# A 64-wide inversion level in three batches instead of four, and a normalisation taken off GpSimd

## The chip, the cores and the metric

The kernel runs on one core of a Trainium2 chip. The metric is device time in microseconds, the median of the runs shown. One further execution was profiled; its trace is what the prediction reads. In the profile, PE is TensorE's matmuls and PEld its weight loads, DVE is VectorE, ACT is ScalarE, POOL is GpSimd.

## The reference

Two transformer layers with a layer norm after each of their four parts. The first layer is grouped-query attention with rotary positions and a gated feed-forward block, over 2 sequences of 1024 tokens of width 256. The second layer is a gated delta rule with 16 heads of width 128, and a feed-forward block with sign weights. The change touches the delta rule alone:

```python
def step(S, inp):
    qt, kt, vt, at, bt = inp
    err = jnp.einsum('bhvk,bhk->bhv', S, kt) - vt
    S = at[..., None, None] * S - bt[..., None, None] * err[..., None] * kt[:, :, None, :]
    o = jnp.einsum('bhvk,bhk->bhv', S, qt)
    return (S, o)
...
mu = o.mean(-1, keepdims=True)
var = ((o - mu) ** 2).mean(-1, keepdims=True)
o = (o - mu) * jax.lax.rsqrt(var + 1e-05) * ln_w + ln_b
g = jax.nn.sigmoid(x @ Wg).reshape(B, T, H, DV)
o = (o * g).reshape(B, T, H * DV)
return o @ Wo
```

## The kernel before

The delta rule is computed in chunks of 128 tokens. Inside a chunk, the recurrence becomes the inverse of a unit triangular 128x128 matrix (`lt` in the code), and between chunks a 128x128 state `M` is carried. The tokens are cut into four stretches of 512 (`HT`), which the code calls halves because two of them make a sequence; the heads are taken in pairs. One **step** `i` of the main loop is one stretch and one pair of heads: 4 chunks x 2 heads, so `U` = 8 triangular matrices. There are 4 x 8 = 32 steps, i = 0 to 31. The attention layer and the first feed-forward block come before them, the last feed-forward block is mixed into the last two steps.

**Order of the work.** A step is 120 units long (`UNIT`). Each part of the work is a generator that yields the unit at which its next piece is due, and `Places.run` always continues the piece that is due first. From step 0 on (`te.strict`), every matmul is tied to the one before it by `te.link`, so TensorE's order is exactly this order. On the other engines a list scheduler at build time picks among the instructions that its own timeline believes ready, by priority: the order of emission, with what stands under `tc.high_priority()` first. What comes out is a fixed queue for each engine. On the chip each engine runs its queue in order.

**The chain, `recur(i)`.** For each of the 4 chunks: at unit 0 of 30 the product `pr` (lines 657 and 661; 661 needs `M`), a copy `prs` on ACT (line 664); at unit 10 the product `pw` with the inverse `lt` (line 672) and the copy `wc` on ACT (line 675); at unit 20 `pm` (line 684), from which DVE makes the new `M` (lines 689 and 691), and `po` (lines 699 and 700), which ACT copies to `o` (line 703). The PSUM pool of the chain has two banks, so the next `pr` also needs DVE to have read `pm`.

**The fill.** Between these pieces TensorE runs the projections of the next steps (`pp`, lines 932 to 934), the transposes and score products, and the inversion: `keys` builds `lt` (product `pkk`, line 338, at units 131 and 141, that is units 11 and 21 of the following step), `blocks` solves the 16x16 blocks, and `levels(i)` puts them together, for two steps (16 matrices) at a time. It runs once every two steps, from step 1 on for i = 2, 4, ... 30: 15 times. One more, `levels(0)`, is emitted ahead of step 0, where the order of matmuls isn't tied yet.

**The last level** joins two 64x64 inverses into one of 128x128. With `A` the first 64 partitions and `Z` the last 64, it is a first product `p3` (rows `A` of the array, columns `Z`; line 469), its negated copy `n3` on ACT (line 471), a second product `p4` (rows `Z`, columns `A`; line 476), and a copy of `p4` into `lt` on ACT (line 477). It is done for one step's 8 matrices after the other's, at units 103, 113, 132 and 142 of the step in which `levels` runs; 132 and 142 lie in the next step. The last four `AT_LEVELS` are these units. `levels` has a PSUM pool of one bank from step 0 on (`"l"`, 1 buffer); `levels(0)` has one with two.

**The normalisation, `finish(i)`.** It runs in the step after. At unit 3 comes the reciprocal root: a few operations on DVE, then 12 small ones on POOL (lines 905 to 908), then `nb` on DVE (line 587). Each of 8 tiles `o` of 128x128 is normalised by one instruction; the string `NORM` says where: `P` POOL, `D` DVE (both line 597), `A` ACT (line 594). At units 41 and 51 TensorE transposes the normalised tiles (`pt`, line 603), first those of head 0 (tiles 0, 2, 4, 6). The last step has a string of its own, `NORM_LAST`.

Of the kernel before, what the change touches and what calls it, by code (L numbers as in the profile page):

```python
# [11 lines left out]
F32 = mybir.dt.float32  # L12
# [3 lines left out]
AF = mybir.ActivationFunctionType  # L16
ALU = mybir.AluOpType
# [3 lines left out]
P = 128  # L21
# [17 lines left out]
U = HP * HC  # L39
# [39 lines left out]
START = 29  # L79
RAW = 4  # L80

NORM, NORM_LAST = 'PDAPDAPD', 'DDADADAA'

UNIT, GAP = 120, 10
AT_ROWS, AT_QUERIES, AT_KC, AT_GATE, AT_GATE_ROWS, AT_SCORES = 1, 31, (42, 52), 61, 70.5, (71, 81)
AT_OUT = 9.5
AT_KEYS, AT_DECAY, AT_TRIANGLE = 91, 113, (131, 141, 146)
AT_BLOCKS, BLOCK_STEP = (44, 52, 145), 2.2
AT_LEVELS = 43, 53, 73, 83, 103, 113, 132, 142
AT_FFN = 24  # L90
AT_FINISH, AT_FINISH_LAST, AT_HALF = (41, 51, 101, 111), (31, 41, 71, 76), ((22, 30, 46), (12, 18, 36))

# [52 lines left out]
def delta_rule(  # L145
# [13 lines left out]
    nc = tc.nc  # L159
# [3 lines left out]
    early = open_pool(left, "dearly", "left", 2)  # L163
# [21 lines left out]
    def bank(pool, tag, name):  # L185
        return pool.tile([P, HT], F32, name=name, tag=tag)
# [43 lines left out]
    st = [dict() for _ in range(B * 2 * NS)]  # L230
# [4 lines left out]
    def place(i):  # L235

        return divmod(i, NS)
# [172 lines left out]
    def levels(i, psum):  # L410

        dd = st[i]["dd"]
        quarter = [slice(q * BL, (q + 1) * BL) for q in range(Q)]
        p0 = bank(*psum, "p0").rearrange("p (u t) -> p u t", t=BL)
        with tc.high_priority():
            for v in range(2 * U):
                for r in quarter:
                    te.link(nc.tensor.matmul(p0[r, v, :], lhsT=lo[r, v, :], rhs=dd[r, v, :], start=True, stop=True))
        n0 = early.tile([P, 2 * U, BL], F32, name="n0", tag="tt", bufs=1)
        with tc.high_priority():  # L420
            nc.vector.scalar_tensor_tensor(
                n0, p0, -1.0, ib.unsqueeze(1).to_broadcast([P, 2 * U, BL]), ALU.mult, ALU.add
            )
        yield AT_LEVELS[1]
        px = bank(*psum, "px").rearrange("p (u t) -> p u t", t=BL)
        with tc.high_priority():
            for v in range(2 * U):
                for r in quarter:
                    te.link(nc.tensor.matmul(px[r, v, :], lhsT=dt[r, v, :], rhs=n0[r, v, :], start=True, stop=True))
        nc.scalar.copy(X[0 : 3 * BL, :, 0:BL], px[0 : 3 * BL])  # L430
        nc.scalar.copy(X[quarter[1], :, BL : 2 * BL], px[quarter[1]])

        with tc.high_priority():
            nc.vector.transpose(dd.rearrange("p u t -> p (u t)"), px.rearrange("p u t -> p (u t)"))
        for n in range(2):
            for r in quarter:
                (nc.gpsimd.tensor_copy if n else nc.scalar.copy)(
                    st[i + n]["lt"][r, :, r], dd[r, n * U : (n + 1) * U]
                )
        yield AT_LEVELS[2]  # L440
        b0, b1, b2, b3 = [slice(q * BL, (q + 1) * BL) for q in range(Q)]
        A, Z = slice(0, 64), slice(64, 128)
        us = [(n * U + u, st[i + n]["lt"], u) for n in range(2) for u in range(U)]
        p1 = bank(*psum, "p1").rearrange("p (u t) -> p u t", t=BL)
        with tc.high_priority():
            for v, lt, u in us:
                te.link(nc.tensor.matmul(p1[b1, v, :], lhsT=lt[b0, u, b1], rhs=X[b0, v, 0:BL], start=True, stop=True))
                te.link(nc.tensor.matmul(p1[b3, v, :], lhsT=lt[b2, u, b3], rhs=X[b2, v, 0:BL], start=True, stop=True))
        n1 = early.tile([P, 2 * U, BL], F32, name="n1", tag="tt", bufs=1)
        for r in (b1, b3):  # L450
            nc.scalar.activation(n1[r], p1[r], AF.Copy, scale=-1.0)
        yield AT_LEVELS[3]
        p2 = bank(*psum, "p2").rearrange("p (u t) -> p u t", t=BL)
        with tc.high_priority():
            for v, lt, u in us:
                te.link(nc.tensor.matmul(p2[b0, v, :], lhsT=n1[b1, v, :], rhs=lt[b1, u, b1], start=True, stop=True))
                te.link(nc.tensor.matmul(p2[b1, v, :], lhsT=lt[b1, u, b1], rhs=n1[b1, v, :], start=True, stop=True))
                te.link(nc.tensor.matmul(p2[b2, v, :], lhsT=n1[b3, v, :], rhs=lt[b3, u, b3], start=True, stop=True))
        nc.vector.tensor_copy(X[b1, :, 0:BL], p2[b1])
        for n in range(2):  # L460
            lt = st[i + n]["lt"]
            nc.scalar.copy(lt[b0, :, b1], p2[b0, n * U : (n + 1) * U])
            nc.scalar.copy(lt[b2, :, b3], p2[b2, n * U : (n + 1) * U])
        for n in range(2):
            yield AT_LEVELS[4 + 2 * n]
            p3 = bank(*psum, "p3").rearrange("p (u t) -> p u t", t=64)
            with tc.high_priority():
                for v, lt, u in us[n * U : (n + 1) * U]:
                    te.link(nc.tensor.matmul(p3[Z, u, :], lhsT=lt[A, u, Z], rhs=X[A, v, :], start=True, stop=True))  # L469
            n3 = early.tile([P, U, 64], F32, name="n3", tag="n3", bufs=1)  # L470
            nc.scalar.activation(n3[Z], p3[Z], AF.Copy, scale=-1.0)
            yield AT_LEVELS[5 + 2 * n]
            p4 = bank(*psum, "p4").rearrange("p (u t) -> p u t", t=64)
            with tc.high_priority():
                for v, lt, u in us[n * U : (n + 1) * U]:
                    te.link(nc.tensor.matmul(p4[A, u, :], lhsT=n3[Z, u, :], rhs=lt[Z, u, Z], start=True, stop=True))  # L476
            nc.scalar.copy(st[i + n]["lt"][A, :, Z], p4[A])

    def pair(m, i):

# [86 lines left out]
    def finish(i, o, m, chunks, places):  # L567
# [5 lines left out]
        if chunks[0] == 0:  # L573
            st[i]["wo"] = []
            for part in range(2):
                t = pools["late"].tile([P, HP, E], F32R, name=f"wo{part}", tag=f"wo{part}", bufs=1)
# [11 lines left out]
        for c in chunks:  # L588
            for h in range(HP):
                n = (c - c1) * HP + h  # L590
                oc, r1 = o[:, c, h, :], rs[:, n : n + 1]
                how = (NORM if i < last else NORM_LAST)[n]
                if how == "A":
                    nc.scalar.activation(oc, oc, AF.Identity, bias=nb[:, n : n + 1], scale=r1)
                else:
                    eng = nc.gpsimd if how == "P" else nc.vector
                    eng.tensor_scalar(oc, oc, m[:, n, 0:1], r1, ALU.subtract, ALU.mult)
        ys = []
        for h in range(HP):
            yield places[h]  # L600
# [12 lines left out]
        for c0 in range(0, nc_, 2):  # L613
            yield places[2 + c0 // 2]
            pf = bank(pools["t"], "t", "pf").rearrange("p (c e) -> p c e", e=E)
            for c in range(2):
                for h in range(HP):
                    t = slice((c0 + c) * P, (c0 + c + 1) * P)
# [10 lines left out]
    def recur(i):  # L629
# [8 lines left out]
        def moments(c):  # L638
            for h in range(HP):
                st6 = pools["late"].tile([P, 6], F32, name="ost", tag="ost")  # L640
                nc.vector.bn_stats(st6, o[:, c, h, :])
                nc.vector.bn_aggr(m[:, c * HP + h, 0:2], st6)
            part = HC // 2 if i == last else HC
            if c % part == part - 1:
                chunks = range(c + 1 - part, c + 1)
                at = i * UNIT + 3 * GAP * (c + 1) + 3
                lines.add(finish(
                    i, o, m[:, chunks[0] * HP : (c + 1) * HP, :], chunks,
                    AT_HALF[c // part] if i == last else AT_FINISH_LAST if i == last - 1 else AT_FINISH,
                ), at, at if i == last else (i + 1) * UNIT)  # L650
# [160 lines left out]
    for i in range(-AHEAD, last + 1):  # L811
        te.strict = i >= 0
        t = i * UNIT
# [4 lines left out]
        if i == -1:  # L818
            drain(keys(3, 0))
            drain(levels(0, (ps_m, "m")))  # L820
            open_late()
# [12 lines left out]
        if i >= 0:  # L834
            lines.add(recur(i), t, chain=True)
            if i % 2 == 0 and i + 2 <= last:
                lines.add(blocks(i + 2, (pools["l"], "l")), t + AT_BLOCKS[0], t)
            if i % 2 == 1 and i + 1 <= last:
                lines.add(levels(i + 1, (pools["l"], "l")), t + AT_LEVELS[0], t)
        hi, s = place(i + AHEAD + 1)  # L840
# [809 lines left out]
```

## Time and profile before

| | |
|---|---|
| runs | median 2069.81 us of 3 (2068.07 to 2072.84) |
| profiled execution | 2075.78 us, of which the span from first to last instruction is 2074.1 us |
| granted TensorE clock, mean over the span | 0.975 |
| PE / PEld busy | 1897.8 us (92%) / 1496.0 us (72%) |
| DVE / ACT / POOL busy | 1493.4 us (72%) / 1269.6 us (61%) / 1035.4 us (50%) |
| step 0 begins / last matmul of the last `levels` starts | 822.7 us / 1920.8 us |

Rows of the timeline are: start, duration (both in us), engine, line, operation, output tile <- input tiles, shape, count, and in brackets the idle time of the engine just before, with what ended it. Buffer numbers are left out of names, so `p3` and `p4` are both `p`, `n3` is `n`, and the blocks of the inverse are `ll`. A float32 matmul shows as two instructions: 8 products are 16 rows.

### The profile page before, as it was taken

What the parts mean: (1) busy time and instruction counts of PE and PEld (TensorE: products, weight loads), DVE (VectorE), ACT (ScalarE), POOL (GpSimd) and SP (SyncE); (2) the same over time, 40 slices, a digit from 0 to 9 for tenths busy, and PEclk for the clock granted to TensorE, in tenths of its full rate; (3) what the DMA queues carried; (4) which work ended last, traced back from release to release, by engine and by line L of the source; (5) the groups of instructions that cost most, each with busy time, mean ns of one, the idle gap of its engine ahead of it and who ended that gap; (6) DMA issues with size and microseconds to landing.
All of it is one profiled execution on the core that took longest, in us unless ns stands there. A gap on an engine that the chain in (4) does not pass through costs nothing.

```text
span 2074.1 us, 49172 instructions
## 1 busy us (share of the span) xinstructions
PE 1897.8 (92%) x18657; PEld 1496.0 (72%) x18657; DVE 1493.4 (72%) x3629; ACT 1269.6 (61%) x2731; POOL 1035.4 (50%) x1539
## 2 busy tenths in 40 slices
PE   5898889999998888899999999998999999999896
PEld 3454455555555777788889888887888888888775
DVE  6755666877757896477786887778678678775576
ACT  1365556576755355567667676766677666676532
POOL 4353333331123453566776656666567676565430
PEclk9999999999999998999999999999999999999997
DMA  5563444442132422443443534444434444443010
GB/s 173 173 185 119 148 127 127 144 135 69 52 76 62 120 74 53 126 129 107 120 132 99 157 99 116 116 122 127 112 114 128 122 115 128 108 132 89 21 41 21
DMA packets 312997, 229.16 MB, mean 110 GB/s; under 512 B 139640, under 2 KB 278904, under 8 KB 312760
## 3 DMA queue, kind: packets, MB, share of 16 engines
q1 hardware_dynamic: 299640, 210.73, 35.0%
q10 hardware_dynamic: 9760, 10.83, 1.6%
q0 software_dynamic: 3360, 4.46, 0.9%
q8 instruction: 147, 2.41, 0.5%
q14 instruction: 90, 0.74, 0.1%
HBM read 171.18 MB, written 51.87 MB: 108 GB/s over the span
## 4 chain that ended last, share of the span: by engine, by line
PE 58%; DVE 13%; ACT 6%; DMA 5%; issue 3%; POOL 2%; SPq 1%; ACTq 0%; POOLq 0%; DVEq 0%
PE pp L932 5%; PE pp L934 4%; PE pp L933 4%; PE ps L1306 4%; PE av L1327 4%; PE ps L1237 3%; PE pkq L506 3%; PE pm L684 2%; DVE at L325 2%; PE pw L672 2%; PE pr L661 2%; PE po L700 2%; PE po L699 2%; PE p L476 2%; PE p L469 2%
## 5 line engine op out<-in xcount | busy, mean ns | idle before, releaser
L1246 DVE TENSOR_REDUCE mx<-ps 128x4 f32<-128x1024 f32 (+1 forms) x320 | 344.3, 1111 | 135.2 <-PE ps L1237 91.2
L1310 ACT ACTIVATE es<-ps 128x512 f32<-128x512 f32 (+1 forms) x608 | 314.0, 577 | 130.2 <-PE ps L1306 119.5
L1306 PE MATMUL ps<-qT,kT 128*128 128x512 f32 (+3 forms) x768 | 221.5, 372 | 21.9 <-ACT es L1310 20.6
L1237 PE MATMUL ps<-kT,qT 128*128 128x512 f32 x576 | 198.8, 419 | 27.8 <-DVE mx L1246 18.7
L1306 PEld LDWEIGHTS ps<-qT,kT 128*128 128x128 f32 x768 | 131.4, 191 | 107.9 <-ACT es L1310 61.5
L1237 PEld LDWEIGHTS ps<-kT,qT 128*128 128x128 f32 x576 | 101.0, 189 | 87.8 <-DVE mx L1246 48.1
L289 ACT ACTIVATE far<-pp,cw 128x509 f32<-128x509 f32 x192 | 133.2, 699 | 47.1 <-DVE v L275 20.8
L1327 PE MATMUL av<-es,vaug 128*32 128x512 f32 (+3 forms) x1536 | 159.4, 503 | 0.2 <-POOL es L1313 0.2
L882 POOL TENSOR_TENSOR wfl<-wf,wfh 128x256 fp32r<-128x256 f32 x80 | 58.6, 734 | 191.0 <-ACT wfh L970 163.0
L1313 POOL TENSOR_SCALAR_AFFINE_SELECT es<-es 128x512 f32<-128x512 f32 x128 | 80.4, 638 | 146.3 <-ACT es L1310 146.1
L275 DVE SCALAR_TENSOR_TENSOR k<-pp,cw,k 128x511 f32<-128x511 f32 (+1 forms) x128 | 92.0, 743 | 46.7 <-ACT k L268 25.0
L275 DVE SCALAR_TENSOR_TENSOR q<-pp,cw,q 128x511 f32<-128x511 f32 (+1 forms) x128 | 93.0, 742 | 45.1 <-ACT q L268 22.2
L292 POOL TENSOR_TENSOR q<-q,far 128x509 f32<-128x509 f32 x64 | 69.4, 1087 | 97.4 <-ACT far L289 97.2
L275 DVE SCALAR_TENSOR_TENSOR v<-pp,cw,v 128x511 f32<-128x511 f32 (+1 forms) x128 | 92.3, 739 | 30.7 <-ACT v L268 18.3
L292 POOL TENSOR_TENSOR k<-k,far 128x509 f32<-128x509 f32 x64 | 78.4, 1227 | 56.8 <-ACT far L289 56.4
L516 POOL TENSOR_TENSOR k<-k,dg 128x508 f32<-128x508 f32 x64 | 81.4, 1271 | 37.9 <-PE pkq L506 32.2
L970 ACT CAST wfh<-wf 128x256 fp32r<-128x256 f32 x80 | 32.4, 406 | 108.0 <-DMA wf<-in_w1k 34.6
L700 PE MATMUL po<-wc,at 128*128 128x128 f32 x512 | 96.6, 275 | 0.0
L664 ACT COPY prs<-pr 128x256 f32<-128x256 f32 x128 | 48.8, 381 | 73.0 <-PE pr L661 64.6
L325 DVE TENSOR_TENSOR_SCAN at<-da,d 128x512 f32<-128x512 f32 x64 | 91.0, 1459 | 0.0
L684 PE MATMUL pm<-wc,kc 128*128 128x128 f32 x448 | 77.1, 295 | 13.0 <-ACT wc L675 12.9
L1327 PEld LDWEIGHTS av<-es,vaug 128*32 128x32 f32 x1536 | 39.1, 110 | 68.2 <-issue 53.8
(314 smaller groups left out, 5942.3 us busy)
## 6 DMA issues: line engine op xcount, KB each, us to landing
wk<-w1k SPq DMA_DIRECT2D x64, 256.0 KB
da<-dec SPq DMA_DIRECT2D x64, 256.0 KB
wv<-w1v SPq DMA_DIRECT2D x64, 256.0 KB
wq<-w1q SPq DMA_DIRECT2D x64, 256.0 KB
dg<-dec SPq DMA_DIRECT2D x64, 256.0 KB
wg<-w1g SPq DMA_DIRECT2D x64, 256.0 KB
wo<-w1o SPq DMA_DIRECT2D x64, 256.0 KB
ad<-avs ACTq DMA_DIRECT2D x32, 256.0 KB
```

What stands on the lines that cost most here:

```text
L275: made = nc.vector.scalar_tensor_tensor(acc[:, d:], pp[:, 0 : HT - d], cw[:, n, hd, KS - 1 - d : KS - d], acc[:, d:], ALU.mult, ALU.add)
L289: made = nc.scalar.activation(far[:, w], pp[:, w], AF.Copy, scale=cw[:, n, hd, 0:1])
L292: nc.gpsimd.tensor_add(acc[:, KS - 1 :], acc[:, KS - 1 :], far[:, w])
L325: nc.vector.tensor_tensor_scan(e, dec, d1.rearrange("p c t -> p (c t)"), 0.0, ALU.mult, ALU.add), taps
L684: te.link(nc.tensor.matmul(pm[:, r], lhsT=st[i]["kc", h][:, c, :], rhs=wc[:, r], start=True, stop=True))
L700: te.link(nc.tensor.matmul(po[:, r], lhsT=st[i]["at", h][:, t], rhs=wc[:, r], start=(M is None), stop=True))
L932: te.link(nc.tensor.matmul(out, lhsT=lhi, rhs=rhi, start=k0, stop=False))
L1237: anchor["mm"] = te.link(nc.tensor.matmul(ps[:, j - j0, :].rearrange("p (g k) -> p g k", k=P), lhsT=q_, rhs=kT[:, :, j * P : (j + 1) * P], ...
L1246: nc.vector.tensor_reduce(mx[:, it, j0 // 2, :], ps[:, 0:n, :].rearrange("p j (g k) -> p g j k", k=P), AX.XY, ALU.max)
L1306: te.link(nc.tensor.matmul(ps[:, g - g0, :], lhsT=kT[:, g, jb * P : (jb + 1) * P], rhs=qT[:, i0 : i0 + w], start=True, stop=True,))
L1310: exps.append(nc.scalar.activation(es[:, g0 : g0 + n, 0:w], ps, AF.Exp, scale=D ** -0.5))
L1327: mm = te.link(nc.tensor.matmul(av[ROW * g : ROW * (g + 1), i0 - ih * 512 : 512], lhsT=vaugs[b][:, jb, kv, :], rhs=es[:, g, 0:w], start=(j ...
```

## The change

It does two things. First, the last level of the inverse is done in three batches at units 103, 113 and 132. The first holds the first products of the one step's 8 matrices, the second holds that step's second products alternating with the other step's first products, and the third holds the other step's second products. In the middle batch both kinds write one PSUM bank, each its own 64 partitions. The copy `n3` is now emitted at the beginning of the next batch instead of the end of its own, and the matmuls no longer stand under `tc.high_priority()`. Second, `NORM` has no `P` any more: of the 8 tiles of a step, DVE takes 4 instead of 3 and ACT 4 instead of 2, and the branch for POOL goes.

```diff
-NORM, NORM_LAST = 'PDAPDAPD', 'DDADADAA'
+NORM, NORM_LAST = 'DADAADAD', 'DDADADAA'
...
-AT_LEVELS = 43, 53, 73, 83, 103, 113, 132, 142
+AT_LEVELS = 43, 53, 73, 83, 103, 113, 132
...
-        for n in range(2):
-            yield AT_LEVELS[4 + 2 * n]
-            p3 = bank(*psum, "p3").rearrange("p (u t) -> p u t", t=64)
-            with tc.high_priority():
-                for v, lt, u in us[n * U : (n + 1) * U]:
+
+        yield AT_LEVELS[4]
+        p3 = p4 = None
+        for n in range(3):
+            if n:
+                yield AT_LEVELS[4 + n]
+                n3 = early.tile([P, U, 64], F32, name="n3", tag="n3", bufs=1)
+                nc.scalar.activation(n3[Z], p3[Z], AF.Copy, scale=-1.0)
+            p3 = p4 = bank(*psum, "p3").rearrange("p (u t) -> p u t", t=64)
+            for u in range(U):
+                if n < 2:
+                    v, lt, _ = us[n * U + u]
                     te.link(nc.tensor.matmul(p3[Z, u, :], lhsT=lt[A, u, Z], rhs=X[A, v, :], start=True, stop=True))
-            n3 = early.tile([P, U, 64], F32, name="n3", tag="n3", bufs=1)
-            nc.scalar.activation(n3[Z], p3[Z], AF.Copy, scale=-1.0)
-            yield AT_LEVELS[5 + 2 * n]
-            p4 = bank(*psum, "p4").rearrange("p (u t) -> p u t", t=64)
-            with tc.high_priority():
-                for v, lt, u in us[n * U : (n + 1) * U]:
+                if n:
+                    lt = st[i + n - 1]["lt"]
                     te.link(nc.tensor.matmul(p4[A, u, :], lhsT=n3[Z, u, :], rhs=lt[Z, u, Z], start=True, stop=True))
-            nc.scalar.copy(st[i + n]["lt"][A, :, Z], p4[A])
+            if n:
+                nc.scalar.copy(st[i + n - 1]["lt"][A, :, Z], p4[A])
...
                 if how == "A":
                     nc.scalar.activation(oc, oc, AF.Identity, bias=nb[:, n : n + 1], scale=r1)
                 else:
-                    eng = nc.gpsimd if how == "P" else nc.vector
-                    eng.tensor_scalar(oc, oc, m[:, n, 0:1], r1, ALU.subtract, ALU.mult)
+                    nc.vector.tensor_scalar(oc, oc, m[:, n, 0:1], r1, ALU.subtract, ALU.mult)
```

## The prediction

> **What bounds the kernel now.** I read the page's busy table and its 40 slices first, then the busy time in stretches of two steps, then the timeline around the last level, then the waits. From the page:
>
> ```profile
> PE 1897.8 (92%) x18657; PEld 1496.0 (72%) x18657; DVE 1493.4 (72%) x3629; ACT 1269.6 (61%) x2731; POOL 1035.4 (50%) x1539
> PE   5898889999998888899999999998999999999896
> PE 58%; DVE 13%; ACT 6%; DMA 5%; issue 3%; POOL 2%; SPq 1%; ACTq 0%; POOLq 0%; DVEq 0%
> ```
>
> PE fills the delta-rule slices (16 to 37) almost wholly, and it has over half of the chain that ended last. By stretches (columns: length, then busy us of PE, PEld, DVE, ACT, POOL, then the granted clock), an undisturbed pair of steps and the worst one:
>
> ```profile
> 970.93:1041.10 70.17, 68.45 (x882) 61.21 (x880) 52.88 (x148) 49.60 (x114) 50.24 (x80) 1.00 0.44 119
> 1402.61:1483.39 80.78, 71.22 (x882) 63.28 (x880) 59.65 (x177) 51.32 (x118) 47.38 (x72) 0.94 0.41 116
> ```
>
> In 70.2 us PE is idle for 1.7; DVE, ACT and POOL have 17 to 21 us to spare. So TensorE time removed here shortens the kernel, as long as the pieces left still cover the chain's copies. The second stretch holds one stall of 7.11 us, where PE waits for normalised tiles.
>
> **The last level.** The matmuls around its four batches in one pair of steps (1326 to 1341 us) follow each other without a gap. First batch and last:
>
> ```profile
> 1326.73 1.14 PE L469 MATMUL p<-X,lt 64*64 64x64 f32 x16
> 1327.80 0.49 PE L699 MATMUL po<-M,q 128*128 128x128 f32 x2
> ...
> 1339.84 1.14 PE L476 MATMUL p<-lt,n 64*64 64x64 f32 x16
> 1340.91 0.33 PE L657 MATMUL pr<-ident,v 128*128 128x128 f32 x1
> ```
>
> A batch keeps the next matmul off for 1.07 us. It also costs about 0.10 on entry: neighbours of one shape start 0.16 to 0.17 before the modelled end of the one ahead, a batch only 0.07 before. So 1.17 us for each of the 60 tied batches, which all show 1.07 to 1.08 and no wait.
>
> *Removed:* one batch per `levels`, 15 x 1.17 = **-17.5 us**.
>
> *Do first and second products run side by side?* `levels(0)`, whose order is free, happens to show the middle batch of the change already:
>
> ```profile
> 791.75 0.27 PE L476 MATMUL p<-lt,n 64*64 64x64 f32 x1
> 791.75 0.27 PE L469 MATMUL p<-X,lt 64*64 64x64 f32 x1
> 791.85 0.22 PE L476 MATMUL p<-lt,n 64*64 64x64 f32 x1
> 791.86 0.22 PE L469 MATMUL p<-X,lt 64*64 64x64 f32 x1
> ...
> 792.82 0.38 PE L1485 MATMUL ph<-fx,w_gate 128*128 128x256 f32 x1
> ```
>
> 32 instructions in 792.82 - 791.75 = 1.07 us, as long as 16 take. There the two products had a bank each, and in the change they share one. For one bank the smaller levels are the row: lines 447 and 448 write two quarters of one bank from two quarters of the rows, 64 instructions in 1.13 us (1316.55 to 1317.68), and lines 456 to 458 put 96 into the same 1.13 us. I take 1.07 to 1.14 (one beat of 0.067 for the two streams to get out of step), **+0.5** (0 to +1.0).
>
> The Trainium skill speaks against this: "TensorEngine Tiling (Array Packing)", Restrictions and Gotchas, says that different row tiles cannot access the same PSUM bank at once. By that rule the middle batch would take twice 1.07, and of the 17.5 us only the entry, 15 x 0.10, would be left. The rows of lines 447 and 448 show otherwise, at least for separate partitions, so I go by them.
>
> *What the removed batch covered.* Unit 142 lay between `pm`/`po` and the next `pr`, which waits for DVE's `M`. In this pair `pm` ends at 1338.1, DVE reads it late, and `pr` comes with 1.5 us to spare:
>
> ```profile
> 1337.38 0.85 DVE L597 TENSOR_SCALAR o<-o,om 128x128 f32<-128x128 f32 x3
> 1338.15 0.75 DVE L275 SCALAR_TENSOR_TENSOR v<-pp,cw,v 128x510 f32<-128x510 f32 x1
> 1338.81 0.60 DVE L691 SCALAR_TENSOR_TENSOR M<-M,ge,pm 128x128 f32<-128x128 f32 x2
> ```
>
> `M` is done at 1339.41; without the batch `pr` could start at 1340.91 - 1.17 = 1339.74. I did this for all 15: seven or eight would wait, 0.05 to 0.50 us each, 1.6 us together. DVE's fourth normalisation is queued before `M`: 0.28 more (three take 0.85), and the sum is 4.1. I take **+3** (1.6 to 4.1). The gap at unit 132 loses nothing: a batch of 1.07 stays there.
>
> *Moved copies.* `n3` and the copy into `lt` stay two each per level (0.59 and 0.58 us on ACT); no DMA moves. `n3` is emitted later, which counts only if the scheduler then queues it behind something; in the waits ACT is found idle and waiting for the first products in 28 of the 30 copies between 880 and 1960, so it was the only thing ready:
>
> ```profile
> ACT n L471 <- PE p L469: 22.4, 28, 1.5
> 1327.91 0.59 ACT L471 ACTIVATE n<-p 64x512 f32<-64x512 f32 x1 [0.79 <-PE p L469]
> 1329.00 0.37 ACT L703 COPY o<-po 128x256 f32<-128x256 f32 x1 [0.49 <-PE po L700]
> ```
>
> It ends at 1328.50 and is needed at 1330.32; 0 here, the price otherwise below. The lost priority means nothing where matmuls are tied; `levels(0)` ends near 797 and its `lt` is first used after 822.7: 0.
>
> **The normalisation.** Per step, 3 x 0.81 = 2.4 us leave POOL; ACT gets 2 x 0.44 (a pair takes 0.88), DVE 0.28. Over 31 steps that is 75 us off POOL, 27 on ACT and 9 on DVE. None of the three is the bound, so only places with a small margin count:
>
> - *The tiles' transposes.* From the end of `nb` (line 587) POOL's three end after 1.5 to 2.5 us. ACT's four would end after its present start (0.2 to 1.6) plus 1.8. The second is later than the transposes want in eight steps: 0.1 to 0.6 us each, 2.8 in all. Since a PE that is late elsewhere no longer waits here, **+1.5** (0 to 2.8).
> - *`M` in the other step of a pair.* Five waits of 0.3 to 0.9 us for `M` are there already; 0.28 more for up to nine of them: **+1** (0 to 2.5).
> - *ACT's queue behind the normalisation.* In the step with `levels`, ACT runs almost without a gap from 1302 to 1313.6, then copies the blocks of the inverse until 1316.0; their product (line 447) starts at 1316.55. 0.88 more, less a gap of 0.32, against a margin of 0.55: about nothing, up to 0.5 in each of 15 levels. **+1.5** (0 to 7).
> - *POOL relieved.* Only two waits of PE name POOL's normalisation between 880 and 1960, and 7.3 of their 8.3 us are the stall:
>
> ```profile
> PEld pt L603 <- POOL o L597: 8.3, 2, 7.3
> 1452.80 2.60 POOL L597 TENSOR_SCALAR o<-o,om 128x128 f32<-128x128 f32 x3
> 1453.80 1.08 PE L603 MATMUL pt<-ident,o 128*128 128x128 f32 x3 [7.11 <-POOL o L597]
> ```
>
> There POOL began its tiles only at 1452.80, since the root's last operation came at 1452.42, and `nb` on DVE stood behind a layer norm until 1453.45. Four tiles on ACT from 1453.64 would end at 1455.4 too. So 0 (0 to -8.6: the stall, and the clock of 0.94 after it, worth some 1.5).
>
> **Sum:** -17.5 + 0.5 + 3 + 0 + 1.5 + 1 + 1.5 + 0 = **-10 us**, on the profiled 2075.78: 2065.8. That execution lay 6 us above the median 2069.81, so the prediction is **2060 us** (-0.5%). With every cost at its low end it is -17.5 and 2052; at its high end -17.5 + 1 + 4.1 + 2.8 + 2.5 + 7 = 0 and 2070. 0.2%, 4.1 us, is about what a measurement can tell from no change.
>
> **Rivals.**
>
> *Slower: `n3` comes late.* Emitted after unit 113, it ranks behind `o`'s copy of unit 110 and what ACT has after that. For the first batch: copy of `o` to 1329.37, `far` and a `silu` to 1330.48, `n3` to 1331.1, against the batch at 1330.32: 0.8 us. For the last: behind `wc`, which ends at 1336.15, `n3` to 1336.74, against 1336.34: 0.4. PE's order is tied, so all behind it waits: 1.2 x 15 = +18, in all +8 and 2078. It decides once `n3` starts later than about 1329.7 in the one place and 1335.7 in the other. For it: the order of emission. Against: the 28 waits of an idle ACT.
>
> *No saving: the bank serialises the pair.* 1.07 instead of 0.03 more in 15 batches: -17.5 + 16 + 7 = +5.5, 2075. Against it stand lines 447, 448 and 456 to 458.
>
> *The queues come out otherwise and the stall of 7.11 us goes:* -10 - 8.6 = -19, 2051; with the costs at their low end, 2044. For it: only one of the three changes of token stretch has such a stall, so a small shift in a queue makes or unmakes it. Against: the root before it and the layer norm aren't touched.
>
> *ACT becomes the limit:* a third of its 27 us added lands on the path beyond what is counted: +9, 2069. Against: 20 us of slack in 70.
>
> **Chances.** Forecast 0.55 (0.47 faster, 0.08 same, since its range reaches 2070); `n3` late 0.15 (0.12 slower, 0.03 same); serialised 0.05 (0.03 slower, 0.02 same); stall gone 0.12 (faster); ACT the limit 0.13 (0.03 faster, 0.06 same, 0.04 slower). Sums: faster 0.62, same 0.19, slower 0.19. The range 2044 to 2078 reaches from the stall gone to `n3` late; the forecast's own is 2052 to 2070.
>
> **What would show it.** Right: L469 and L476 alternating in a batch of about 1.1 us with 32 instructions, three batches per level; an undisturbed pair of steps near 69.5 us; PE's busy time down by some 17; waits of lines 657 and 661 for `M` up by 2 to 4 us. Wrong: a batch of 2.1; PE waiting at line 476 for ACT's copy at the new line of `n3`; waits of line 603 for ACT's normalisation over 5 us; a new stall of several us where a stretch of tokens ends.

## The result: 2074.5 us, 0.25% slower, and the profile after

| | before | after |
|---|---|---|
| median of 20 runs each, side by side | 2068.30 us (2062.54 to 2073.27) | 2074.46 us (2067.79 to 2083.95) |
| ratio of after to before | | 1.0025, 95% interval 1.0014 to 1.0036 |
| profiled execution / span | 2075.78 / 2074.1 us | 2069.76 / 2068.0 us |
| step 0 to the last matmul's end, profiled execution | 1243.4 us | 1243.1 us |

The time lies inside the predicted range (2044 to 2078), but on the other side of no change: 2060 was forecast. The profiled execution of after lies 4.7 us below its median and that of before 7.5 us above its own, so the two spans mustn't be compared. Step 0 begins 5.8 us earlier in after, which is 5.0 us ahead at 660 us already, long before `levels(0)`, the only piece ahead of step 0 that the change touches. Everything below is measured from step 0 on, where these two executions are equal.

The page of after, the lines that answer to those of before:

```profile
span 2068.0 us, 49156 instructions
PE 1885.6 (91%) x18657; PEld 1480.3 (72%) x18657; DVE 1511.7 (73%) x3660; ACT 1289.6 (62%) x2793; POOL 954.9 (46%) x1446
PE   5898989999998887999999999999999999999886
PE 42%; DVE 23%; ACT 9%; DMA 6%; issue 3%; POOL 3%; SPq 1%; DVEq 0%; ACTq 0%; POOLq 0%
```

PE is busy 12 us less, where some 17 were predicted, and POOL is relieved by 80 us, about as foreseen (75). DVE is busy 18 us more, where 9 were booked, and its share of the chain that ended last has gone from 13% to 23%, PE's from 58% to 42%: in this execution the end is set more often by something that DVE does. The timeline of PE around a middle batch of after:

```profile
1039.23 0.27 PE L476 MATMUL p<-X,lt 64*64 64x64 f32 x1
1039.23 0.27 PE L479 MATMUL p<-lt,n 64*64 64x64 f32 x1
1039.34 0.22 PE L476 MATMUL p<-X,lt 64*64 64x64 f32 x1
1039.34 0.22 PE L479 MATMUL p<-lt,n 64*64 64x64 f32 x1
...
1040.31 0.44 PE L660 MATMUL pr<-ident,v 128*128 128x128 f32 x2
```

First products (now line 476) and second (479) start in pairs, and all 32 are through in 1040.31 - 1039.23 = 1.08 us, in one bank. That part does what it says. Now the busy time by stretch. The first line is the pair of steps from before's undisturbed stretch (4 and 5), the second is steps 2 to 29 as a whole; the third is the same whole for before, 896.04 to 1913.17:

```profile
968.99:1040.30 71.31, 68.08 (x884) 60.20 (x880) 54.87 (x147) 50.60 (x118) 45.19 (x74) 1.00 0.42 118
891.06:1907.47 1016.41, 965.03 (x12401) 856.56 (x12398) 787.12 (x2182) 723.84 (x1624) 596.16 (x954) 0.99 0.42 119
```

```profile
896.04:1913.17 1017.13, 971.66 (x12399) 867.32 (x12398) 769.74 (x2154) 706.55 (x1568) 668.41 (x1038) 0.99 0.42 119
```

The pair takes 71.31 us where it took 70.17; 69.5 was predicted. PE is busy 6.6 us less over the 28 steps and idle 5.9 us more (51.4 against 45.5), although before's 45.5 hold the stall of 7.11 us and after has only 1.6 and 0.9 in its place. Where the idle time is, the waits of PE between 880 and 1960 say (total, times, longest):

```profile
PE pm L687 <- ACT wc L678: 9.1, 10, 1.2
PE pr L660 <- ACT o L706: 5.7, 10, 1.6
PE pt L606 <- DVE y L610: 5.5, 3, 1.8
PE pr L664 <- DVE M L692: 5.5, 11, 0.8
PE pr L660 <- DVE M L694: 4.4, 4, 1.5
...
PE pt L606 <- DVE o L600: 2.5, 2, 1.6
...
PE pt L606 <- ACT o L598: 1.6, 4, 0.4
```

The three rows of `pr` hold the new waiting: 15.6 us, where all rows of `pr` in before make 4.5 in the same window (3.1, 1.1 and 0.3). The wait of `pm` for `wc` was there before (10.7), and the waits of `pt` for normalised tiles are small.

**Where the waits stand.** I cut each pair of steps at the start of each of its eight chunks and took the mean over 13 pairs (2-3 to 26-27; after 28 the last block mixes in). The batch that went lay in the first chunk of the even step. Of the 15.4 us that PE waits for `pr` in these pairs, 10.6 come right behind that chunk; it was 0.0 there in before. The first two chunks of the even step take 16.22 us in before **and 16.23 us in after**: the whole saving of the batch is lost on the spot. I use this length, and the time from `pm`'s end to the new `M`, as the measure in all that follows.

**What makes `M` late.** The timeline of after, steps 4 to 5, in the middle of that first chunk, with the rows that matter here in order of time:

```profile
974.87 0.71 PE L687 MATMUL pm<-wc,kc 128*128 128x128 f32 x4
975.17 1.88 DVE L600 TENSOR_SCALAR o<-o,om 128x128 f32<-128x128 f32 x4
975.29 1.65 ACT L598 ACTIVATE o<-o,om 128x128 f32<-128x128 f32 x4
975.32 1.14 POOL L292 TENSOR_TENSOR v<-v,far 128x509 f32<-128x509 f32 x1 [0.82 <-ACT far L289]
976.97 0.67 DVE L339 SCALAR_TENSOR_TENSOR lt<-pkk,at 128x508 f32<-128x508 f32 x1
977.31 0.36 ACT L706 COPY o<-po 128x256 f32<-128x256 f32 x1
977.56 0.73 DVE L275 SCALAR_TENSOR_TENSOR v<-pp,cw,v 128x510 f32<-128x510 f32 x1
977.73 0.33 PE L660 MATMUL pr<-ident,v 128*128 128x128 f32 x1 [0.80 <-ACT o L706]
978.22 0.47 DVE L692 COPY M<-pm 128x128 f32<-128x128 f32 x2
978.55 0.49 PE L664 MATMUL pr<-M,k 128*128 128x128 f32 x2 [0.49 <-DVE M L692]
```

and the same place of before:

```profile
976.50 0.71 PE L684 MATMUL pm<-wc,kc 128*128 128x128 f32 x4
976.91 2.44 POOL L597 TENSOR_SCALAR o<-o,om 128x128 f32<-128x128 f32 x3
976.92 0.94 DVE L597 TENSOR_SCALAR o<-o,om 128x128 f32<-128x128 f32 x3
978.35 0.48 DVE L689 COPY M<-pm 128x128 f32<-128x128 f32 x2
979.31 2.13 POOL L292 TENSOR_TENSOR v<-v,far 128x509 f32<-128x509 f32 x2
```

In before POOL has its three tiles beside DVE's three; only then, at 979.31, does it add `far` to `v` (line 292, part of the projections' convolution). In after POOL has no tiles, and the addition starts at 975.32, in the middle of DVE's four. Those take 1.88 us. Three took 0.94 in before, and one takes 0.33, so four should take about 1.25. One by one they take 340, 1109, 335 and 336 ns. The row of all such tiles (shortest, middle and longest in ns) shows the same: the longest is 3.5 times the middle one.

```profile
L600 DVE TENSOR_SCALAR o<-o,om x130: 329/336/1192, 862.7 to 2018.1; 128x128 f32<-128x128 f32 x130
```

I call a DVE instruction **held** when it is one of these tiles, or the small `nb` ahead of them (0.17 us as a rule), and takes over 0.6 us. In the first chunk of the 13 pairs, before has no held one. After has one in every pair, 0.75 to 1.19 us long, always beside an addition of `far` to `v`: a tile in 11 pairs, `nb` in 2. `M` is done 2.66 us after `pm`'s end on average; it was 1.34. On ACT, `o`'s copy, which frees the bank that `pr` writes, stands behind four tiles instead of two. And with the batch of unit 142 gone, 1.07 us of other work are missing in front of `pr` just there.

**Theory:** POOL's addition moves into the slot that its tiles leave and blocks DVE, and the batch that covered a late `M` is gone; each alone is cheap, both together cost the saving. **Rivals:** DVE's fourth tile is enough; or the place of the third batch (132 or 142) is; or ACT's longer queue.

### The profile page after: what moved, and what is told of

It is laid out like the page before. It is cut to its first block, busy times and chain, and to the rows that moved or that the text cites. A ratio compares the mean times of both kernels' runs of the same rounds, so it can differ in the third digit from the quotient of the medians.

```text
span 2068.0 us, 49156 instructions
## 1 busy us (share of the span) xinstructions
PE 1885.6 (91%) x18657; PEld 1480.3 (72%) x18657; DVE 1511.7 (73%) x3660; ACT 1289.6 (62%) x2793; POOL 954.9 (46%) x1446
## 4 chain that ended last, share of the span: by engine, by line
PE 42%; DVE 23%; ACT 9%; DMA 6%; issue 3%; POOL 3%; SPq 1%; DVEq 0%; ACTq 0%; POOLq 0%
PE ps L1309 4%; PE av L1330 4%; PE ps L1240 3%; PE pp L935 3%; DVE at L325 3%; DVE k L275 3%; PE pp L937 3%; PE pp L936 3%; PE pkq L510 2%; DVE v L275 2%; PE pr L664 2%; DVE o L600 1%; PE pm L687 1%; DVE xtok L625 1%; PE pw L675 1%
## 5 line engine op out<-in xcount | busy, mean ns | idle before, releaser
L292 POOL TENSOR_TENSOR v<-v,far 128x509 f32<-128x509 f32 x64 | 70.1, 1096 | 77.6 <-ACT far L289 59.7
L664 PE MATMUL pr<-M,k 128*128 128x128 f32 x448 | 83.3, 281 | 6.3 <-DVE M L692 5.5
```

What stands on the lines that cost most here:

```text
L292: nc.gpsimd.tensor_add(acc[:, KS - 1 :], acc[:, KS - 1 :], far[:, w])
L664: te.link(nc.tensor.matmul(pr[:, r], lhsT=st[i]["k", h][:, t], rhs=M[:, r], start=False, stop=True))
```

## The experiments

Ratios are against executions of before beside them, with their intervals; their median was 2070 to 2075 us. The quotient of two medians can differ from the ratio by 0.2%. "Two chunks" is the mean length of the first two chunks of the even step (before 16.22, after 16.23), "`M`" the mean time from `pm`'s end to `M` there, and "held" the number of the 13 pairs whose first chunk has a held instruction (before 0, after 13).

**1 and 2. Each part alone.** `e1_levels` is the change with the old normalisation (its branch for POOL is back too), `e2_norm` the new normalisation with the old four batches.

```diff
 e1_levels, against after          e2_norm, against before
-NORM = 'DADAADAD'                -NORM = 'PDAPDAPD'
+NORM = 'PDAPDAPD'                +NORM = 'DADAADAD'
```

> The level in three batches alone; the normalisation as before (three tiles on POOL). Theory 'normalisation': the change loses what the three batches gain because POOL's tiles went to DVE and ACT; then this run is 0.4 to 0.6% faster than before (8 to 12 us), and the waits of TensorE for pr (lines 657/661 before) stay near the 4.5 us of before, at most 9. Rival 'cover': the gain is lost in the gap between pm and pr where the fourth batch stood; then this run is within 0.15% of before and the waits for pr are at 12 us or more, as after the change (15.6 us).

> The normalisation of the change alone (four tiles on DVE, four on ACT, none on POOL); the level in four batches as before. 'Normalisation': 0.6 to 0.9% slower than before (12 to 18 us), since the whole change is 0.25% slower and the batches gain 0.4 to 0.6%. 'Cover': 0 to 0.3% slower, because the fourth batch still covers M's lateness.

| | ratio | two chunks | `M` | held | waits of `pr` behind the first chunk |
|---|---|---|---|---|---|
| batches alone | 0.9921 [0.9893, 0.9950], 2058.32 us | 15.35 | 1.70 | 0 | 1.2 |
| normalisation alone | 1.0009 [0.9992, 1.0026], 2073.14 us | 16.29 | 2.28 | 13 | 0.8 |
| both (after) | 1.0025 [1.0014, 1.0036] | 16.23 | 2.66 | 13 | 10.6 |

Run 1 came out on the side of the theory "normalisation", run 2 on that of "cover", so neither is the whole answer: the parts don't add. -0.8% and +0.1% would make -0.7%; both together are +0.25%, so the combination costs about 0.95%, some 19 us. The normalisation alone also has the addition hold DVE, in all 13 pairs (`nb` in 10, a tile in 3), and makes `M` late (2.28), but there the batch of unit 142 still hides it. The stretch of steps 2 to 29 of batches alone:

```profile
897.87:1897.42 999.55, 956.40 (x12401) 851.46 (x12397) 765.82 (x2154) 705.05 (x1568) 670.14 (x1038) 1.00 0.43 121
```

It is 16.9 us shorter than in after, on DVE 21.3 us less busy. That is more than a fourth tile in 28 steps is worth: 28 x 0.33 = 9.

**3. POOL's time kept filled.** Three useless POOL instructions per step, of the kind and size of the old tiles.

```diff
+                if i < last and n in (0, 3, 6):
+                    spare = pools["late"].tile([P, P], F32, name="spare", tag="spare", bufs=1)
+                    nc.gpsimd.tensor_scalar(spare, ident, m[:, n, 0:1], r1, ALU.subtract, ALU.mult)
```

> The whole change, and POOL does three extra operations of the same form as its former normalisations (128x128 from a constant into a spare tile that nobody reads) right after the root. Theory 'POOL's gap': with its three tiles gone, POOL starts the addition of far to v 2 us earlier, beside DVE's normalisation, and one of DVE's four then takes 1.19 us instead of 0.33; then the spare work brings the longest of them back to about 0.5 us, and the time to 0.2 to 0.6% below that of the change (which is +0.25% against before). Rival 'load': DVE's fourth and ACT's two further tiles themselves are the cost; then it is as slow as the change, +0.15 to +0.4% against before.

1.0018 [0.9999, 1.0038], 2075.58 us, two chunks 16.21: as the change. This tells nothing for or against, because the scheduler put an addition of `far` between the spare instructions: it still stood beside DVE's tiles in the first chunk of all 13 pairs and held one in 8; the longest tile took 1232 ns.

**4 and 5. The third batch at unit 142 instead of 132,** with the old normalisation (`e4_levels_142`) and with the new one (`e5_change_142`).

```diff
-AT_LEVELS = 43, 53, 73, 83, 103, 113, 132
+AT_LEVELS = 43, 53, 73, 83, 103, 113, 142
```

> As the run with the level alone, but the third batch at unit 142 instead of 132: it covers the gap between pm and pr, as the fourth batch did, and leaves the one between pw and pm with pkk alone. If M's lateness is what costs ('cover'), it is 2 to 6 us faster than the run with the batch at 132. If wc's copy needs the cover more, TensorE waits 0.7 to 1.4 us for wc in each of 15 levels, as it does now in the step without a batch there, and this is 8 to 15 us slower than the run with the batch at 132.

> The whole change, with the third batch at unit 142 instead of 132, where the fourth batch stood. Theory 'cover x queue': the new normalisation makes M and o about 1 us later in the step's first chunk, and that shows only because the batch between pm and pr is gone (pr waits 10.6 us in 13 pairs of steps at that place after the change, 1.2 with the batches alone, 0.8 with the normalisation alone). With a batch back in that gap the wait there falls below 3 us and the run is 0.5 to 0.8% faster than before (2054 to 2060 us). Rival 'load': DVE's and ACT's longer queues cost wherever the batches stand; then it stays within 0.2% of the change, 0 to +0.4% against before.

Old normalisation: 0.9930 [0.9903, 0.9956], no different from 132, where 2 to 6 us less or 8 to 15 more were expected. New normalisation: 0.9987 [0.9973, 1.0001], 2070.46 us; the waits of `pr` fall from 10.6 to 2.4 us as expected, and the two chunks to 15.58, but the gain over the change is 0.4% where 0.75 to 1 was expected. So cover at that one place is somewhat under half of the matter. DVE is still held in 13 of 13 pairs and `M` isn't earlier (3.13). That number compares with batches alone at 142, which have 2.14: with the batch behind `pm` instead of ahead of it, the count starts at an earlier `pm`.

**6. Three tiles on DVE, five on ACT.**

```diff
-NORM = 'DADAADAD'
+NORM = 'DADAADAA'
```

> The whole change, but tile 7 goes to ACT: three tiles on DVE as before the change, five on ACT. If DVE's fourth tile, queued ahead of M, is the cost, pr's wait at that place (10.6 us in 13 pairs) falls by a quarter to a half (0.28 to 0.6 us each in those that wait) and the run is 0.1 to 0.3% faster than the change. If ACT's tiles, queued ahead of o's copy, are the cost, it is 0.1 to 0.3% slower than the change.

1.0029 [1.0013, 1.0046], 2077.66 us, two chunks 16.13, `M` 2.37, the waits of `pr` 11.5: neither of the two expected changes of time. The addition still holds DVE in 13 of 13 pairs. As the tile went to ACT, whose queue got longer, this run alone doesn't clear the fourth tile; the table under 7 does.

**7. The same useless work as in 3, and `v`'s additions on POOL tied behind its last instruction.**

```diff
...
-            nc.gpsimd.tensor_add(acc[:, KS - 1 :], acc[:, KS - 1 :], far[:, w])
+            made_far = nc.gpsimd.tensor_add(acc[:, KS - 1 :], acc[:, KS - 1 :], far[:, w])
+            if m == "v" and spared:
+                after(made_far, spared[-1])
```

> As the run with three spare operations on POOL, and now the additions of far to v are tied behind the last of them in POOL's queue (in that earlier run one of the two still stood between them). Theory 'POOL beside DVE': while POOL adds far, one of DVE's normalisations takes 1.2 us instead of 0.33; with the addition behind the spare work, no normalisation on DVE is over 0.6 us, M is 0.7 us earlier, pr's wait at the first chunk falls from 10.6 us in 13 pairs to 3 to 6, and the run is 0.3 to 0.6% faster than the change, that is 0.1 to 0.4% faster than before. Rival: the normalisations' number alone makes M late; then the wait stays at 9 to 11 us and the time within 0.15% of the change.

0.9963 [0.9949, 0.9977], 2063.74 us: 0.6% faster than the change, with the same tiles on DVE and ACT and more work on POOL. From 3 it differs by the tie alone, and the two chunks go from 16.21 to 15.55 us. The same place in its timeline:

```profile
977.27 2.82 POOL L605 TENSOR_SCALAR spare<-ident,om 128x128 f32<-128x128 f32 x3
977.85 1.11 DVE L602 TENSOR_SCALAR o<-o,om 128x128 f32<-128x128 f32 x4
980.06 1.08 POOL L292 TENSOR_TENSOR v<-v,far 128x509 f32<-128x509 f32 x1
```

DVE's four tiles take 1.11 us instead of 1.88, `M` comes 1.84 after `pm` instead of 2.66, and DVE is busy 16.8 us less over steps 2 to 29 (770.3), doing the same work. No pair has a held instruction in its first chunk. With the runs before it, this separates the tile from the addition (`M`, two chunks):

| | addition kept away (held 0 of 13) | addition beside (held 13 of 13) |
|---|---|---|
| three tiles on DVE | 1.70, 15.35 (batches alone) | 2.37, 16.13 (experiment 6) |
| four tiles on DVE | 1.84, 15.55 (this one) | 2.66, 16.23 (after) |

The addition costs 0.7 to 0.8 us in either row, the fourth tile 0.1 to 0.3 in either column (ACT has two, four or five tiles in these runs). So the rival of the fourth tile falls. Part of the gain is paid back: PE now waits 12.6 us at the output projection `pf` for DVE's addition to `xtok`, against 3.1 in after.

**8 and 9. The same aim without useless work:** `v`'s copies `far` on ACT tied behind ACT's last tile, with the third batch at 132 (`e8_far_behind_norm`) and at 142 (`e9_far_norm_142`).

```diff
+            if m == "v" and normed:
+                after(made, normed[-1])
...
-                    nc.scalar.activation(oc, oc, AF.Identity, bias=nb[:, n : n + 1], scale=r1)
+                    normed.append(nc.scalar.activation(oc, oc, AF.Identity, bias=nb[:, n : n + 1], scale=r1))
```

> The whole change, with no spare work; in ACT's queue, v's far is tied behind the last of ACT's four normalisations, so that POOL can add it only when the normalisations are over. Theory 'POOL beside DVE': the run with spare work and the addition behind it was 0.6% faster than the change; without the spare work this comes out the same, 0.4 to 0.7% faster than the change (0.15 to 0.45% faster than before), and the longest normalisation on DVE outside the changes of token stretch is under 0.6 us. Rival: in that run the spare work, or the planner's other choices beside it, made the difference; then it is within 0.2% of the change.

> As the last one, with the third batch at unit 142. If lost cover and POOL beside DVE are the two halves of one loss, each cure leaves little for the other: 0 to 0.3% faster than the last one, and at the best level with the batches alone (0.8% faster than before). If they add, another 0.4% on top of the last one.

1.0203 [1.0181, 1.0225] and 1.0204 [1.0186, 1.0221]: 2% slower, a miss. `far` is the copy that frees the projection's bank, and the next projection now waits for it. In the waits of PE, between 880 and 1960:

```profile
PE pp L937 <- ACT far L289: 45.0, 13, 4.5
```

That is about the whole 2%, and so the time says nothing on the theory. The first chunk does: without any useless work, no tile of steps 2 to 29 takes over 346 ns in either run, none of the 13 pairs has a held instruction, and in 8 `M` comes 1.91 us after `pm`, the two chunks take 15.68 us and the waits of `pr` behind the first are 5.3 us instead of 10.6. What has to be kept back is POOL's addition, not the copy ahead of it.

**10. The blocking by itself.** A small kernel that leaves out the network and only puts DVE instructions of 128x128 beside POOL's.

```diff
...
+    for dve, other, times in (
+        (one, None, 0), (one, pool_scalar, 12), (one, pool_add, 10),
+        (two, None, 0), (two, pool_scalar, 12), (two, pool_add, 10), (None, pool_scalar, 12), (None, pool_add, 10),
+    ):
...
```

> Not the network: DVE's normalisation form (tensor_scalar 128x128, two column operands, SBUF to SBUF) 24 times alone, beside 12 of POOL's tensor_scalar 128x128, and beside 10 of POOL's additions 128x509; then the same with a DVE product of two tensors. Theory: alone 0.28 to 0.34 us each; beside POOL's tensor_scalar under 0.45; beside POOL's addition some of them take about 1.1 us, as long as one addition. Rival: beside the addition they stay under 0.5 us, and the 1.19 us in the kernel came from something else.

Its timeline (of one execution), 24 of DVE's normalisations in each row: alone, beside POOL's scalar instructions, beside POOL's additions, and those additions:

```profile
3.47 9.14 DVE L34 TENSOR_SCALAR ddst<-dsrc,sc 128x128 f32<-128x128 f32 x24
13.39 10.61 DVE L34 TENSOR_SCALAR ddst<-dsrc,sc 128x128 f32<-128x128 f32 x24
24.79 16.83 DVE L34 TENSOR_SCALAR ddst<-dsrc,sc 128x128 f32<-128x128 f32 x24
...
24.63 11.56 POOL L40 TENSOR_TENSOR pacc<-pacc,psrc 128x509 f32<-128x509 f32 x10
```

24 tiles take 9.14 us alone, 1.5 us more beside twelve scalar instructions of POOL, but 7.7 us more beside ten of its additions. Beside the additions the longest tile takes 1128 ns, alone each takes 346; the additions keep to 1083 to 1087 ns. Beside the scalar instructions every second tile takes about 476 ns, a little over the 450 expected, and those instructions go from 795 to 927. So POOL's two-tensor addition stops DVE and isn't slowed itself, while POOL's scalar instruction costs DVE 0.13 us: the old tiles on POOL did DVE little harm, and the addition in their place does.

**11. Both cures:** the tie of 7 and the place of 5.

> The whole change with both cures: the spare work on POOL with v's far additions tied behind it, and the third batch at unit 142. If lost cover and POOL beside DVE together make up the whole loss against the batches alone, this comes to 0.6 to 0.9% faster than before (2052 to 2060 us), and pr waits less than 3 us at the first chunk of 13 pairs. Rival: something of the new normalisation is left that neither cures; then it stays at 0.2 to 0.5% faster, where the first cure alone came to.

0.9884 [0.9862, 0.9906], **2051.91 us**: 1.2% faster than before and 1.4% faster than the change, although POOL still does the useless work. The two chunks take 15.14 us, 1.07 less than in before, no pair has a held instruction, and 0.4 us of waits for `pr` are left behind the first chunk. The loss against batches alone is made up, and the time is better than the 0.6 to 0.9% expected. Against batches alone with the same place of the batch (experiment 4, two chunks 15.05), steps 2 to 29 are 8.6 us shorter here; the two pairs of steps 8-9 and 16-17 make 9.3 of it (71.63 and 74.07 us instead of 75.75 and 79.27), so what is gained on top lies in these two pairs and not in the first chunk. Its steps 2 to 29, where PE is idle for 35.1 us:

```profile
898.46:1887.23 988.77, 953.66 (x12399) 853.79 (x12396) 766.71 (x2176) 722.33 (x1623) 669.50 (x1037) 0.99 0.44 122
```

**12 and 13. The collision put into batches alone (1).** One useless POOL instruction ahead of POOL's tiles: a two-tensor product of 128x384 (`e12_add_beside`) or a scalar instruction of 128x128 (`e13_scalar_beside`).

```diff
...
+            beside = nc.gpsimd.tensor_mul(spare, spare, spare)                                              (12)
+            beside = nc.gpsimd.tensor_scalar(spare[:, 0:128], ident, m[:, 0, 0:1], rs[:, 0:1], ALU.subtract, ALU.mult)   (13)
...
+                    if how == "P":
+                        after(made, beside)
```

> The batches alone, the normalisation as before, and POOL does one useless product of two tensors 128x384 (about 0.8 us) right after the root, ahead of its three tiles: it stands beside DVE's three normalisations. Theory 'POOL beside DVE': it holds one of them for 0.5 to 0.9 us, M comes that much later, pr's wait at the first chunk rises from 1.2 us in 13 pairs to 5 to 10, and the run is 0.2 to 0.5% slower than the batches alone (0.3 to 0.6% faster than before instead of 0.8%). Rival: another 0.8 us in POOL's queue does the same whatever its form; then the next run is as slow.

> As the last one, but the useless operation is of the form of POOL's normalisation (tensor_scalar 128x128, also about 0.8 us). Theory: it does not hold DVE; within 0.15% of the batches alone, pr's wait at most 4 us in 13 pairs. Rival: as slow as the last one, within 0.1%.

1.0109 [1.0087, 1.0131] and 1.0101 [1.0080, 1.0121]: both 1.8 to 1.9% slower than batches alone, whatever the form, so my expectation of the time missed. In the small the form matters as the theory has it: the product holds DVE in 10 of 13 pairs (0.61 to 0.87 us), the scalar instruction in none; `M` is at 2.10 us and 1.65 (1.70 without either), and `pr` waits 3.8 us and 1.2, where 5 to 10 and at most 4 were expected. But the time goes elsewhere, in the waits of PE of 12 and of 13, one line each:

```profile
PE pf L945 <- DVE xtok L635: 25.9, 14, 3.1
```

```profile
PE pf L945 <- DVE xtok L635: 32.3, 14, 3.9
```

One place in the timeline of experiment 13:

```profile
1529.55 3.17 DVE L325 TENSOR_TENSOR_SCAN at<-da,d 128x512 f32<-128x512 f32 x2
1532.64 0.66 DVE L635 TENSOR_TENSOR xtok<-pf,xtok 128x512 f32<-128x512 f32 x1
1533.36 0.38 PE L945 MATMUL pf<-wo,yh 128*128 128x256 f32 x1 [3.02 <-DVE xtok L635]
```

Here the list scheduler has put two scans ahead of DVE's addition to `xtok`, which frees `pf`'s only bank. All waits of `pf` over 1 us in steps 2 to 29 (8 in 12, 10 in 13) stand behind a scan in this way; batches alone have none over 0.5 us. Of the 56 additions in these steps, 11 and 12 come straight behind a scan in 12 and 13, and 4 in batches alone. This is a second effect, apart from the holding: with a POOL instruction more, DVE's fixed queue comes out in another order, and each order has its own waits. It adds 22 and 28 us of the 40 by which steps 2 to 29 are longer than in batches alone.

## Why the prediction was wrong

- **The step that failed** is the cover of unit 142, "+3 (1.6 to 4.1)", together with "POOL relieved", "0 (0 to -8.6)". I laid the missing batch over before's times of `M` and added 0.28 for the fourth tile. For the old normalisation that held: in batches alone the two chunks get shorter by 0.87 us of the expected 1.17 - 0.03 = 1.14, so the cost is 0.27 x 15 = 4 us. But I took `M`'s time as fixed but for the tile, while the other part of the change moved it. In after the two chunks get no shorter, so the cost is 1.14 x 15 = 17 us: the term is short by 13 to 14 us, and that carries the forecast across zero.
- **Why `M` moved:** POOL's freed slot was booked at "0 or a gain", with no loss possible. I followed who waits for POOL, and not what POOL would do in the freed time. Of the 1.0 us between 1.70 (batches alone) and 2.66, 0.8 go when the addition is kept out of the way (1.84 in experiment 7); the fourth tile, for which 0.28 was booked, and the order are the rest.
- **A page spoke of it.** The Trainium skill, "SBUF — State Buffer", section "SBUF: two separate sides", says that VectorE and GpSimd share a pair of ports under an exclusive lock, and that the later of a GpSimd instruction and a VectorE instruction which uses that pair waits for the whole of the other. The 1109 ns of one tile beside an addition of 1.14 us in after, and the 7.7 us in experiment 10, agree. Two things don't: it draws no line between GpSimd's one-tensor and two-tensor instructions, and beside twelve scalar ones 24 tiles lost only 1.5 us in all; and the additions never waited in turn, ten of them taking 11.56 us with VectorE's tiles beside them and without.
- **Right: the batch's value and the shared bank.** The middle batch takes 1.08 us (+0.5 was booked, 0.03 each), and batches alone come out at -0.8%; the terms that concern them, -17.5 + 0.5 + 1.6, make -15.4 us, -0.7%. The two chunks bear 0.87 x 15 = 13 us of that out; in the profiled executions some 6 more are the stall of 7.11 us, which batches alone happens not to have (74.55 us for the pair of steps that took 80.78). With the batch at 142 (experiment 4) the stall is there again (79.27), the two chunks take 15.05, and the time is the same. So the size is right in part by luck: the stall, on which nothing was booked here, comes and goes. The forecast's -10 for the whole would have needed the parts to add.
- **Right in size: the normalisation alone.** +1.5 + 1 + 1.5 = +4 us, 0.2%, were booked; measured is +0.1% [-0.1, +0.3]. That the cost lies in the booked waits isn't shown: in the profile of experiment 2, PE is idle 45.1 us over steps 2 to 29, against 45.5 in before.
- **Right: `n3` isn't late.** Line 471 is the releaser of 0.2 us of PE's waits in all of after. **Right: `pt`.** The waits for ACT's tiles are 1.6 us in all, for DVE's 2.5.
- **ACT as the limit: only in part.** `o`'s copy behind four tiles is the releaser of 5.7 us of `pr`'s waits (3.0 in batches alone), but with the same four tiles on ACT experiment 11 has 0.7. So ACT's tiles add to the loss while `M` is late, and are not the bound.
- **The stall of 7.11 us** did shrink, to 1.6 and 0.9, as one rival had it, and its pair of steps from 80.78 to 76.39 us. Most of that was given back: steps 2 and 3 take 77.93 us instead of 74.89, at a clock of 0.96 instead of 1.00. The clock falls twice there, the second time behind a wait of 1.8 us for `pt`. Experiment 5 has the same wait there at a clock of 1.00 (74.63 us), so why the clock falls stays open.
- **What stays open.** Of the 19 us that the combination costs, 12 to 13 are the two chunks; the rest is spread over other places, and I can't assign it. Every edit also gives the engines new queue orders, as 12 and 13 show, so the cause is shown for the first chunk and not for each microsecond of a run's time. Of the 16.9 us by which steps 2 to 29 of after are longer than those of batches alone, PE is idle for 8.2; for the other 8.6 it is busy longer with the same number of matmuls (965.0 against 956.4), in part in the stretches of the lower clock.

## What to carry to other kernels

Of two edits, one may gain and the other be nearly free, and together the gain is lost: where one takes away cover and the other may delay what was covered, run them apart and then together. Before an operation is taken off an engine that isn't the bound, look at what stands behind it in that engine's queue, where it will land, and whom it meets there; in this kernel the two-tensor work on GpSimd beside short VectorE instructions of the chain was the thing to avoid. Taking a fill batch off TensorE saves its time only where nothing late stands behind it.

## What the hardware showed that I had not expected

In experiment 10 a GpSimd addition of 128x509 takes 1.08 us whether VectorE works or not, but a VectorE normalisation of 128x128 that meets it takes up to 1.13 us instead of 0.35 (in after up to 1.19 instead of 0.34). The two-tensor product on VectorE is held as well (up to 1.20 us against 0.29). So is an instruction as small as `nb` (128x8): in after it took 1.03 us once beside the addition, instead of 0.17. GpSimd's one-tensor scalar instruction lengthened a VectorE instruction by 0.13 us, and got longer by as much itself (795 to 927 ns).
